# A CIN kernel on one core: joint squares for the first four chunks, second factors by shift matmuls for two chunks, another order of loads and of M

## The chip, the core and the metric

The kernel runs on one core of a Trainium2 chip. The metric is device time in microseconds (us), smaller is better. A time is one execution of the whole program; the profile is of one such execution.

## The reference

The input x has 1024 samples of 64 fields with 16 values each. Three layers of a compressed interaction network follow, all in float32. Without the dead branches the reference is:

```python
x0 = x; h = x; xs = []
for i in range(3):
    z = jnp.einsum('bfe,bge->bfge', x0, h)           # all products of fields
    z = z.reshape(Bn, f0 * fh, e)
    y = jnp.einsum('oc,bce->boe', Ws[i], z) + bs[i][None, :, None]
    if i != 2:
        x_i, h = y[:, :64, :], y[:, 64:, :]          # half is output, half goes on
    else:
        x_i, h = y, y
    xs.append(x_i)
pooled = jnp.sum(jnp.concatenate(xs, axis=1), axis=2)   # sum over the 16 values
out = pooled @ fc_w.T + fc_b                            # 256 -> 1
```

W0 is 128 x 4096, W1 and W2 are 128 x 4096 too. The output has 1024 numbers.

## The kernel before

**Tiling.** The 1024 samples are cut into 32 chunks of 32 samples; a chunk has 512 columns (32 samples by 16 values). The products of two fields are formed with the pair of fields on 128 partitions. Since a product of fields is symmetric, 16 tiles of 128 pairs and one tile of squares are enough. Tile t = 4j + i multiplies `xa` (the fields shifted by i, 128 partitions x 4 x 512) with `xb[j]` (the fields shifted by 4(j+1) and, in the lower half, by 16 more). `product(c, j)` forms four tiles `z` at once in one VectorE (DVE) instruction of 128 x 2048; in the last j, ScalarE (ACT) then overwrites a part of one tile with squares (line 220). A few products go to GpSimd (POOL).

**Weights.** Only half of W0 (64 output rows) is needed for h1; the output of the last layers is linear, so the kernel multiplies fc_w into W2 first (v2, lines 378 to 398), then v2 into W1 (the matrix M, `pm`, lines 404 to 414), writes M to HBM (`md`) and reads it back in skewed forms (`ms`), so that DVE can add the two halves of each symmetric pair into `w_all` (line 499). `w_all` holds for each tile 64 columns for h1 (W0) and 64 for M. For a chunk after the first four, TensorE (PE) contracts both at once (128 columns, 512 wide, `contract`, line 256). The first four chunks come before M is there: PE contracts them with the h1 columns first (`half_contract(c, 0, j)`, line 291: 64 columns, the chunk's two halves of 256 columns in two column tiles) and with the M columns later (`half_contract(c, 1, j)`).

**The head.** `HEAD = [2, 3, 0, 1]`, and c0, c1, c2, c3 stand for these four chunks in this order. The last two of them, `KEPT = [0, 1]`, keep their products in SBUF and get their second contraction right after the head; the first two are loaded and multiplied again later. Nothing is scheduled by a planner: `manual_schedule` keeps the order of the program text on each engine, and each engine runs its instructions in order. Loads are issued in the text's order on one queue, SyncE's (SP); DMAs issued on ACT are named in the text.

In the head before the change:

- For c0, the second factors `xp` come from eight small matmuls with a shift matrix (line 189), 64x64 tiles of 512 columns, into PSUM. For c1 they are loaded from HBM as `xb` (1 MB), and ACT copies three of the four to PSUM (line 178).
- c0's first product is one instruction for tile 0 and one for tiles 1 to 3; POOL forms the product j = 1 of c0 and j = 3 of c1.
- W0's two halves are added by DVE (`h1_weights`, line 339). For j = 0 and 1, ACT first copies one half to PSUM (line 355).
- Each chunk has a fifth step `half_contract(c, 0, NJ)` of the remaining squares: ACT squares 64 partitions (`squares`, line 224), and two matmuls with 64 rows add them to h1. Then ACT copies h1 with its bias to `hb` (`keep_h1`, line 297). For the kept chunks ACT also prepares the last tile and xx (`last_tile`, lines 224, 230 and 239) between c1 and c2.
- The order of PE's work is: c0; first quarter of c1; v2's first step (`pv`); fourth quarter of c1; v2's second step (`pt`); second and third quarters of c1; `pm`; squares of c1; c2; c3; then the kept chunks with M.

SP's loads are issued as: xa of c0 (in two parts), W0 (in two parts), xb and xa of c1, W2, xa and xb of c2, W1, and, once c0's buffer is free, xa and xb of c3.

The PSUM tags are `acc` (four banks), `y` and `set` (two each). `zp` has 12 buffers of `z`; `xp` has three of `xa` and of `xb`.

Of the kernel before, what the change touches and what calls it, by code (L numbers as in the profile page):

```python
# [36 lines left out]
F32 = mybir.dt.float32  # L37
AF = mybir.ActivationFunctionType
# [3 lines left out]
F = 64  # L42
# [15 lines left out]
FIRST = 4  # L58
SQ = slice(96, 128)
# [3 lines left out]
def cin_kernel(ctx, tc, xra, xrb, wh, w0r, w1h, w2t, wx1, wx0, vec, out):  # L63
    nc = tc.nc
# [26 lines left out]
    fc2, bh1, bh2 = vs[:, 0:1], vs[:, 1:2], vs[0:64, 2:3]  # L91
    bcol, fcol, fcb = vs[:, 3:5], vs[:, 5:7], vs[0:2, 7:8]
    w0ds, fcr = vs[:, 8:72], vs[:, 72:200]
# [4 lines left out]
    bd = const_tile("bd", [128, 128])  # L98
    nc.gpsimd.memset(bd, 0.0)  # L99

    def keep_clock(n):
        pw = ps.tile([128, 128], F32, tag="acc", name=f"pw_{n}", bufs=4)
        for _ in range(n):
            nc.tensor.matmul(pw, bd, bd, start=True, stop=True)  # L104

    keep_clock(6)

    shift = const_tile("shift", [128, 96])
    nc.gpsimd.memset(shift, 0.0)
    for base in (0, 64, -64):  # L110
        nc.gpsimd.affine_select(
            out=shift, in_=shift, compare_op=ALU.not_equal, fill=1.0, base=base,
# [15 lines left out]
    w_all = const_tile("w_all", [128, NT + 1, 192])  # L128
# [7 lines left out]
    def load_xa(c, at=slice(0, NI)):  # L136
        if c not in xas or at.start == 0:
            xas[c] = xp.tile([128, NI, N], F32, tag="xa", name=f"xa_{c}")
        nc.sync.dma_start(
            out=xas[c][:, at, :],  # L140
            in_=bass.AP(
                tensor=xra.tensor, offset=c * XR * N + at.start * N,
                ap=[[N, 128], [1, (at.stop - at.start) * N]],
            ),
        )

    def load_xb(c):
# [14 lines left out]
    nc.sync.dma_start(out=w0t[:, 0, :], in_=wh)  # L162
    nc.sync.dma_start(out=w0t[:, 1:NJ, :], in_=w0r)
    w0s = [w0t[:, j, :].rearrange("p (i v g) -> p i v g", v=2, g=F) for j in range(NJ)]
    xb0 = xp.tile([128, NJ, N], F32, tag="xb", name=f"xb_{c0}")[:, 0, :]
    load_xb(c1)
    load_xa(c1)
    for k in range(2):
        nc.sync.dma_start(out=w2s[k], in_=w2t[k])
    load_chunk(c2)  # L170
    nc.sync.dma_start(out=w1s, in_=w1h)

    def to_psum(src, tag, name):
        t = ps.tile(list(src.shape), F32, tag=tag, name=name, bufs=4 if tag == "acc" else 2)
        nc.scalar.copy(t, src)
        return t

    xbs[c0] = [
        ps.tile([128, N], F32, tag=tag, name=f"xp_{c0}_{j}", bufs=4 if tag == "acc" else 2)
        for j, tag in enumerate(("y", "y", "set", "acc"))
    ]
    for j in (0, 2):
        for r in range(2):
            for h in range(2):
                at = 4 * (j + r + 1) + 16 * h
                nc.tensor.matmul(  # L189
                    xbs[c0][j + r][halves[h]], shift[halves[r], at : at + F],  # L190
                    xas[c0][halves[r], 0, :], start=True, stop=True,
                )
    keep_clock(8)


# [1 line left out]
    hb = const_tile("hb", [128, NF, N // 2])  # L197
    accs, uus, zs, ys, parts = {}, {}, {}, {}, {}

    def new_acc(c, n=N):  # L200
        if c == NCH - 1:
            parts[c] = [
                (ps.tile([128, H2], F32, tag=tag, name=f"acc_{c}_{n}", bufs=bufs), cols)
                for n, (tag, bufs, cols) in enumerate(
                    (("acc", 4, slice(0, H2)), ("set", 2, slice(H2, N)))
                )
            ]
            return
        accs[c] = ps.tile([128, n], F32, tag="acc", name=f"acc_{c}", bufs=4)

    def product(c, j, first=0, last=NI, engine=nc.vector):
        if first == 0:
            zs[c, j] = z_tile(f"z_{c}_{j}")
        at = slice(first, last)
        engine.tensor_tensor(  # L215
            zs[c, j][:, at, :], xas[c][:, at, :],
            xbs[c][j].unsqueeze(1).to_broadcast([128, last - first, N]), ALU.mult,
        )
        if j == NJ - 1:
            nc.scalar.activation(zs[c, j][SQ, 0, :], xas[c][SQ, 0, :], AF.Square)  # L220

    def squares(c):
        zls[c] = xp.tile([128, N], F32, tag="zl", name=f"zl_{c}", bufs=4)
        nc.scalar.activation(zls[c][0:64], xas[c][0:64, 0, :], AF.Square)  # L224

    def last_tile(c):

        if c < FIRST:
            squares(c)
            nc.scalar.copy(zls[c][64:128], xas[c][64:128, 0, :])  # L230
        else:
            if c % 4 == 0:
# [51 lines left out]
    def half_contract(c, part, j):  # L284

        cols = slice(part * F, (part + 1) * F)
        rows = slice(0, F) if part == 0 and j == NJ else slice(0, 128)
        for t in (NT,) if j == NJ else [j * NI + i for i in tiles(j)]:
            z = zls[c] if t == NT else zs[c, j][:, t % NI, :]
            for n in range(2):  # L290
                nc.tensor.matmul(  # L291
                    accs[c][halves[n]], w_all[rows, t, cols], z[rows, n * H2 : (n + 1) * H2],
                    start=(t == 0), stop=(t == NT),
                )

    def keep_h1(c):
        nc.scalar.activation(hb[:, HEAD.index(c), :], accs[c], AF.Identity, bias=bh1)

    def uu_tile(k):
        if k not in uus:  # L300
# [37 lines left out]
    def h1_weights(j, other=None):  # L338
        nc.vector.tensor_tensor(  # L339
            w_all[:, j * NI : (j + 1) * NI, 0:64], w0s[j][:, :, 0, :],  # L340
            w0s[j][:, :, 1, :] if other is None else other, ALU.add,
        )


    new_acc(c0, H2)
    squares(c0)
    nc.vector.tensor_copy(w_all[0:32, NT, 0:64], w0ds[0:32])
    product(c0, 0, 0, 1)
    product(c0, 0, 1, NI)
    nc.scalar.copy(xb0, xbs[c0][1])  # L350
    xbs[c0][1] = xb0
    product(c0, 1, engine=nc.gpsimd)
    w0p = ps.tile([128, 2, NI, F], F32, tag="set", name="w0p")
    for j in range(2):
        nc.scalar.copy(w0p[:, j], w0s[j][:, :, 1, :])
        h1_weights(j, w0p[:, j])
    product(c0, 2)
    h1_weights(2)
    nc.vector.memset(w0s[3][SQ, 0, 1, :], 0.0)
    h1_weights(3)  # L360
    for j, tag in enumerate(("y", "y", "acc")):
        xbs[c1][j] = to_psum(xbs[c1][j], tag, f"xp_{c1}_{j}")
    product(c0, 3)
    for j in range(NJ + 1):
        half_contract(c0, 0, j)


    for j in range(NJ - 1):
        product(c1, j)
    product(c1, NJ - 1, engine=nc.gpsimd)  # L370
    keep_h1(c0)
    squares(c1)
    load_chunk(c3)
    new_acc(c1, H2)
    half_contract(c1, 0, 0)


    v2r = flat_tile("v2r")[:, 0:1024].rearrange("p (n c) -> p n c", n=2)
    v2t = const_tile("v2t", [128, F])
    for n in range(2):  # L380
        pv = ps.tile([128, 512], F32, tag="set", name=f"pv2_{n}")
        for k in range(4):
            nc.tensor.matmul(  # L383
                pv[32 * k : 32 * k + 32], fv2, w2s[n][:, k * 512 : (k + 1) * 512],
                start=True, stop=True,
                tile_position=(0, 32 * k),
            )
        nc.scalar.copy(v2r[:, n, :], pv)

    half_contract(c1, 0, 3)  # L390


    pt = ps.tile([128, F // 4, 4], F32, tag="acc", name="pt", bufs=4)
    v2q = v2r.rearrange("p n (s o) -> p (n s) o", o=F)
    for q in range(F // 4):
        for to in halves:
            nc.tensor.matmul(pt[to, q, :], v2q[:, q, :], pick, start=True, stop=True)  # L397
    nc.scalar.copy(v2t, pt.rearrange("p q k -> p (q k)"))
    half_contract(c1, 0, 1)

    half_contract(c1, 0, 2)


    m_sb = z_tile("m_sb")
# [8 lines left out]
    for m in (0, 2, 1, 3):  # L413
        nc.scalar.copy(m_sb[:, m, :], pms[m])  # L414

    half_contract(c1, 0, NJ)

# [20 lines left out]
    )  # L438


    keep_h1(c1)
    squares(c2)
    for c in KEPT:
        last_tile(c)

    new_acc(c2, H2)
    for j in range(NJ):
        product(c2, j)
    for j in range(NJ + 1):
        half_contract(c2, 0, j)  # L450


# [27 lines left out]
        read_rows(slice(1, NJ), queue, half)  # L480


    keep_h1(c2)
    new_acc(c3, H2)
    for j in range(NJ):
        product(c3, j)
    for j in range(NJ + 1):
        half_contract(c3, 0, j)

    for j in range(1, NJ):  # L490
# [7 lines left out]
        at = slice(j * NI, (j + 1) * NI)  # L498
        nc.vector.tensor_tensor(w_all[:, at, 64:128], ms[:, 0, at], ms[:, 1, at], ALU.add)  # L499

    keep_h1(c3)


    for j in range(NJ):
# [7 lines left out]


    for c in KEPT:
        new_acc(c, H2)
        for j in range(NJ):
            half_contract(c, 1, j)

# [214 lines left out]
```

## Time and profile before

| what | us |
|---|---|
| median of three runs | 494.91 |
| lowest, highest | 494.75, 495.42 |
| run with the profile | 494.79 |
| span in that profile | 493.0 |
| first product of c2 starts on DVE | 24.63 |
| second contraction of the kept chunks starts on PE | 47.34 |
| chunk 4 starts on PE | 61.31 |

The span goes from the first to the last instruction. The page gives each engine's busy time; the timeline lists instructions in order of time, those alike that follow each other as one row, with the start, the length, and in brackets how long the engine had been idle and what ended that. PE shows two records for each of these float32 matmuls. The end of a matmul in a record is modelled and overlaps the next start, so starts are what is compared. The DMA engines moved 401 to 423 GB/s between 8.45 and 30.58 us. The granted TensorE clock is 1.0 throughout.

### The profile page before, as it was taken

Reading aid. Unit: us, or ns where it says so; the run is one execution under the profiler, and the core shown is the slowest. Engines: PE = TensorE matmul, PEld = TensorE weight load, DVE = VectorE, ACT = ScalarE, POOL = GpSimd, SP = SyncE. Lnnn points to the kernel's source line nnn. Section 1 sums busy time; section 2 is a strip of 40 time slices with the busy share of each in tenths; the row PEclk is TensorE's granted clock in tenths of the full one; section 3 lists DMA queues with packets and bytes.
Section 4 is the critical chain, followed back from the end, with each engine's and each line's share of the span. In section 5 each row is a group of like instructions: output and inputs, shape, how many; then the busy total and the mean of one; then the engine's idle time right before and its main releaser. Section 6 shows DMA issues by size and latency. Waiting matters only on the chain.

```text
span 493.0 us, 4322 instructions
## 1 busy us (share of the span) xinstructions
PE 485.9 (99%) x1804; PEld 229.5 (47%) x1804; DVE 369.1 (75%) x232; ACT 93.0 (19%) x161; POOL 11.4 (2%) x20
## 2 busy tenths in 40 slices
PE   8998999999999999999999999999999999999996
PEld 5555644344644344443444444443444434444474
DVE  4795599998889988898768677776877676780311
ACT  3343012022111131212110021112011121010001
POOL 5300000000000000000000000000000000000000
PEclk9999999999999999999999999999999999999999
DMA  8986994174444453547133444333344430000000
GB/s 341 418 268 150 414 419 183 55 283 175 170 171 170 170 215 127 191 191 281 72 126 163 171 170 169 112 143 109 150 170 171 170 149 21 1 0 0 0 1 1
DMA packets 14243, 79.65 MB, mean 162 GB/s; under 512 B 3756, under 2 KB 4428, under 8 KB 4944
## 3 DMA queue, kind: packets, MB, share of 16 engines
q1 hardware_dynamic: 13084, 78.10, 40.9%
q10 hardware_dynamic: 1140, 1.29, 1.0%
q8 instruction: 14, 0.23, 0.2%
q14 instruction: 5, 0.04, 0.0%
HBM read 77.74 MB, written 1.64 MB: 161 GB/s over the span
## 4 chain that ended last, share of the span: by engine, by line
PE 94%; ACT 2%; DVE 1%; DMA 1%; ACTq 0%; SPq 0%; issue 0%
PE acc L256 78%; PE acc L291 10%; PE acc L275 3%; PE acc L266 2%; DMA w0t<-in_w0r 1%; DVE z L215 1%; ACT m_sb L414 0%; PE po L586 0%; PE y L324 0%; PE pv L383 0%; PE pt L397 0%; ACT zl L224 0%; ACT zl L230 0%; ACTq L432 0%; DVE w_all L339 0%; ACT xx L239 0%
## 5 line engine op out<-in xcount | busy, mean ns | idle before, releaser
L256 PE MATMUL acc<-z,w_all 128*128 128x512 f32 (+1 forms) x928 | 387.6, 579 | 0.0
L215 DVE TENSOR_TENSOR z<-xa,xb 128x2048 f32<-128x2048 f32 x128 | 287.6, 2285 | 46.7 <-PE acc L256 37.9
L256 PEld LDWEIGHTS acc<-z,w_all 128*128 128x128 f32 x928 | 175.6, 190 | 209.9 <-issue 206.3
L220 ACT ACTIVATE z<-xa 32x512 f32<-32x512 f32 x34 | 21.3, 626 | 320.1 <-DVE z L215 317.3
L318 DVE SCALAR_TENSOR_TENSOR uu<-acc,vs,q 64x512 f32<-64x512 f32 (+1 forms) x29 | 21.2, 732 | 61.3 <-ACT q L317 61.0
L291 PE MATMUL acc<-z,w_all 128*64 128x256 f32 x512 | 58.1, 381 | 2.1 <-ACT z L220 1.3
L291 PEld LDWEIGHTS acc<-z,w_all 128*64 128x64 f32 x512 | 35.9, 137 | 24.1 <-issue 4.1
L317 ACT COPY q<-acc 64x512 f32<-64x512 f32 (+1 forms) x29 | 16.4, 565 | 36.5 <-PE acc L256 22.9
L331 DVE TENSOR_REDUCE acc<-uu 128x64 f32<-128x1024 f32 (+3 forms) x20 | 20.5, 1026 | 0.4
L239 ACT COPY xx<-xa 64x512 f32<-64x512 f32 x32 | 19.6, 613 | 0.4
L235 ACT ACTIVATE sq<-xa 32x512 f32<-32x512 f32 x28 | 17.6, 628 | 4.3 <-DMA xa<-in_xra 3.6
L215 DVE TENSOR_TENSOR z<-xa,xp 128x2048 f32<-128x2048 f32 (+2 forms) x7 | 13.5, 1976 | 1.3 <-PE xp L189 1.3
L280 PE MATMUL y<-xx,bd 64*64 64x512 f32 x56 | 13.6, 604 | 0.0
L275 PE MATMUL acc<-xx,v1w 64*64 64x512 f32 (+1 forms) x58 | 13.5, 587 | 0.0
L327 DVE SCALAR_TENSOR_TENSOR uu<-y,cx,xx 128x512 f32<-128x512 f32 x16 | 11.3, 745 | 0.3
L215 POOL TENSOR_TENSOR z<-xa,xb 128x2048 f32<-128x2048 f32 x2 | 9.1, 4558 | 5.7 <-ACT xb L350 3.0
L266 PE MATMUL acc<-sq,w_sq 32*128 32x512 f32 (+1 forms) x58 | 8.0, 623 | 0.0
L275 PEld LDWEIGHTS acc<-xx,v1w 64*64 64x64 f32 x58 | 3.6, 132 | 8.9 <-issue 8.8
L104 PE MATMUL pw<-bd 128*128 128x128 f32 x28 | 5.0, 347 | 1.0 <-POOL bd L99 1.0
L104 PEld LDWEIGHTS pw<-bd 128*128 128x128 f32 x28 | 4.5, 251 | 1.8 <-POOL bd L99 1.0
L499 DVE TENSOR_TENSOR w_all<-ms 128x256 f32<-128x256 f32 x4 | 1.6, 424 | 4.8 <-DMA ms<-md 4.8
L266 PEld LDWEIGHTS acc<-sq,w_sq 32*128 32x128 f32 x58 | 2.6, 183 | 5.4 <-issue 5.3
(62 smaller groups left out, 66.6 us busy)
## 6 DMA issues: line engine op xcount, KB each, us to landing
xb<-in_xrb SPq DMA_DIRECT2D x33, 1024.0 KB, 6.9
xa<-in_xra SPq DMA_DIRECT2D x33, 1024.0 KB, 4.8
w<-in_w2t SPq DMA_DIRECT2D x2, 1024.0 KB, 12.4
w1s<-in_w1h SPq DMA_DIRECT2D x1, 1024.0 KB
w1x<-in_wx SPq DMA_DIRECT2D x1, 1024.0 KB, 9.6
w0x<-in_wx SPq DMA_DIRECT2D x1, 1024.0 KB, 10.1
xa<-in_xra SPq DMA_DIRECT2D x1, 768.0 KB, 4.7
w0t<-in_w0r SPq DMA_DIRECT2D x1, 768.0 KB, 6.4
```

Of the source, the lines that this page charges most:

```text
L215: engine.tensor_tensor(zs[c, j][:, at, :], xas[c][:, at, :], xbs[c][j].unsqueeze(1).to_broadcast([128, last - first, N]), ALU.mult,)
L220: nc.scalar.activation(zs[c, j][SQ, 0, :], xas[c][SQ, 0, :], AF.Square)
L235: nc.scalar.activation(sqs[c // 4][at : at + 32], xas[c][0:32, 0, :], AF.Square)
L239: nc.scalar.copy(xxs[c // 2][to], xas[c][to, 0, :])
L256: nc.tensor.matmul(acc_c, w_all[:, t, w_cols(c)], zs[c, j][:, i, cols], start=(t == 0 and c % 4 < 2), stop=(t == NT - NI and c % 4 >= 2),)
L266: nc.tensor.matmul(acc_c, w_sq[at, w_cols(c)], sqs[first // 4][at, cols], start=(r >= 2), stop=(r < 2), tile_position=(32 * r, 0),)
L275: nc.tensor.matmul(acc_c[q], v1w[rows], xxs[k][rows, cols], start=False, stop=(c % 4 < 2), skip_group_check=True,)
L280: nc.tensor.matmul(ys[k][rows], bd[rows, rows], xxs[k][rows], start=True, stop=True)
L291: nc.tensor.matmul(accs[c][halves[n]], w_all[rows, t, cols], z[rows, n * H2 : (n + 1) * H2], start=(t == 0), stop=(t == NT),)
L317: nc.scalar.copy(q[h, cols], acc_c[64 - h.start : 128 - h.start])
L318: nc.vector.scalar_tensor_tensor(uu[:, cols], acc_c[h], bh1[h], q[h, cols], ALU.add, ALU.mult)
L331: nc.vector.tensor_reduce(acc[rows, of, k, half], uus[k][rows, of, E * half.start : E * half.stop].rearrange("p k (b e) -> p k b e", e=E), ...
```

## The change

- The squares of the four head chunks are no longer a fifth step of each. ACT squares 32 partitions of each chunk into one quarter of a shared tile, `sq_head` (`head_square`), and after c3's first contraction eight matmuls with 32 rows and 64 columns each (`keep_h1`), at row tile 32r and column tile 64n, add them to all four h1 sums. The four copies to `hb` follow there, and then the kept chunks' `last_tile`. The h1 sums stay in the four `acc` banks until then; the kept chunks' second sums use tag `y`.
- c1's second factors come from shift matmuls too, placed after c0's first quarter, in PSUM tiles of tags `y` and `set`. The load of c1's xb is gone; ACT copies one factor to SBUF for POOL. c1's xa is loaded in two parts.
- W1 is loaded before c2's xa and xb.
- v2's first step stands ahead of c1's first quarter, and `pm` after c1's first and fourth quarters, ahead of the second and third.
- c0's product j = 0 is cut into tiles 0, 1 and 2 to 3, with `h1_weights(0)` in between. ACT copies a half of W0 to PSUM for all four j, the last two into `misc`, the bank in which `keep_clock` runs.
- Without use, and removed: the copy of `w0ds` into `w_all`, and the case of 64 rows in `half_contract`.

```diff
-    xb0 = xp.tile([128, NJ, N], F32, tag="xb", name=f"xb_{c0}")[:, 0, :]
-    load_xb(c1)
-    load_xa(c1)
+    xb_gps = xp.tile([128, NJ, N], F32, tag="xb", name="xb_gps")
+    load_xa(c1, slice(0, 1))
+    load_xa(c1, slice(1, 4))
     for k in range(2):
         nc.sync.dma_start(out=w2s[k], in_=w2t[k])
+    nc.sync.dma_start(out=w1s, in_=w1h)
     load_chunk(c2)
-    nc.sync.dma_start(out=w1s, in_=w1h)
...
+    sq_head = xp.tile([128, N], F32, tag="zl", name="sq_head", bufs=4)
+    h1_accs = {}
+
+    def head_square(c):
+        at = 32 * HEAD.index(c)
+        nc.scalar.activation(sq_head[at : at + 32], xas[c][0:32, 0, :], AF.Square)
...
+    def keep_h1():
+        for r, c in enumerate(HEAD):
+            at = slice(32 * r, 32 * r + 32)
+            for n in range(2):
+                nc.tensor.matmul(
+                    h1_accs[c][halves[n]], w0ds[at], sq_head[at, n * H2 : (n + 1) * H2],
+                    start=False, stop=True, tile_position=(32 * r, 64 * n),
+                )
+        for c in HEAD:
+            nc.scalar.activation(
+                hb[:, HEAD.index(c), :], h1_accs[c], AF.Identity, bias=bh1
+            )
...
-    product(c0, 0, 0, 1)
-    product(c0, 0, 1, NI)
...
+    product(c0, 0, 0, 1)
+    product(c0, 0, 1, 2)
+    nc.scalar.copy(w0o[0], w0s[0][:, :, 1, :])
+    h1_weights(0, w0o[0])
+    product(c0, 0, 2, NI)
+    nc.scalar.copy(w0o[1], w0s[1][:, :, 1, :])
+    h1_weights(1, w0o[1])
     product(c0, 2)
-    h1_weights(2)
-    nc.vector.memset(w0s[3][SQ, 0, 1, :], 0.0)
-    h1_weights(3)
-    for j, tag in enumerate(("y", "y", "acc")):
-        xbs[c1][j] = to_psum(xbs[c1][j], tag, f"xp_{c1}_{j}")
+    for j in (2, 3):
+        nc.scalar.copy(w0o[j], w0s[j][:, :, 1, :])
+    nc.vector.memset(w0o[3][SQ, 0, :], 0.0)
+    for j in (2, 3):
+        h1_weights(j, w0o[j])
+    half_contract(c0, 0, 0)
+
+    head_acc(c1)
+    for j, tag in ((0, "y"), (1, "y"), (3, "set"), (2, "set")):
+        shifted(c1, j, tag)
+    shift_pair(c1, (0, 1))
+    shift_pair(c1, (3, 2))
+    nc.scalar.copy(xb_gps[:, 1, :], xbs[c1][3])
+    xbs[c1][3] = xb_gps[:, 1, :]
+    head_square(c1)
+
     product(c0, 3)
-    for j in range(NJ + 1):
+    load_chunk(c3)
+    for j in range(1, NJ):
         half_contract(c0, 0, j)
...
-    keep_h1(c0)
-    squares(c1)
-    load_chunk(c3)
-    new_acc(c1, H2)
-    half_contract(c1, 0, 0)
...
-    half_contract(c1, 0, 3)
+    half_contract(c1, 0, 0)
...
-    half_contract(c1, 0, 1)
-
-    half_contract(c1, 0, 2)
+    half_contract(c1, 0, 3)
...
-    half_contract(c1, 0, NJ)
+    for j in (1, 2):
+        half_contract(c1, 0, j)
...
-    keep_h1(c1)
-    squares(c2)
-    for c in KEPT:
-        last_tile(c)
-
-    new_acc(c2, H2)
+    head_square(c2)
+    head_acc(c2)
     for j in range(NJ):
         product(c2, j)
-    for j in range(NJ + 1):
+    for j in range(NJ):
         half_contract(c2, 0, j)
...
-    keep_h1(c3)
+    keep_h1()
+    for c in KEPT:
+        last_tile(c)
...
     for c in KEPT:
-        new_acc(c, H2)
+        new_acc(c, H2, "y")
```

More of the change, by code (lines that the diff above doesn't have):

```diff
@@ L99, in cin_kernel @@
     nc.gpsimd.memset(bd, 0.0)
+    misc = ps.tile([128, N], F32, tag="acc", name="misc", bufs=4)
     def keep_clock(n):
-        pw = ps.tile([128, 128], F32, tag="acc", name=f"pw_{n}", bufs=4)
         for _ in range(n):
-            nc.tensor.matmul(pw, bd, bd, start=True, stop=True)
+            nc.tensor.matmul(misc[:, 0:128], bd, bd, start=True, stop=True)
     keep_clock(6)
@@ L164, in cin_kernel, with shifted, shift_pair @@
     w0s = [w0t[:, j, :].rearrange("p (i v g) -> p i v g", v=2, g=F) for j in range(NJ)]
-    xb0 = xp.tile([128, NJ, N], F32, tag="xb", name=f"xb_{c0}")[:, 0, :]
-    load_xb(c1)
-    load_xa(c1)
+    xb_gps = xp.tile([128, NJ, N], F32, tag="xb", name="xb_gps")
+    load_xa(c1, slice(0, 1))
+    load_xa(c1, slice(1, 4))
     for k in range(2):
         nc.sync.dma_start(out=w2s[k], in_=w2t[k])
+    nc.sync.dma_start(out=w1s, in_=w1h)
     load_chunk(c2)
-    nc.sync.dma_start(out=w1s, in_=w1h)
[L176 to L186, printed above, removed]
+    def shifted(c, j, tag):
+        xbs.setdefault(c, {})[j] = ps.tile(
+            [128, N], F32, tag=tag, name=f"xp_{c}_{j}", bufs=4 if tag == "acc" else 2
+        )
+    def shift_pair(c, js):
+        for r, j in enumerate(js):
             for h in range(2):
-                at = 4 * (j + r + 1) + 16 * h
+                at = 4 * (j + 1) + 16 * h
                 nc.tensor.matmul(
-                    xbs[c0][j + r][halves[h]], shift[halves[r], at : at + F],
-                    xas[c0][halves[r], 0, :], start=True, stop=True,
-                )
+                    xbs[c][j][halves[h]], shift[halves[r], at : at + F],
+                    xas[c][halves[r], 0, :], start=True, stop=True,
+                )
+    for j, tag in enumerate(("y", "y", "set", "acc")):
+        shifted(c0, j, tag)
+    shift_pair(c0, (0, 1))
+    shift_pair(c0, (2, 3))
     keep_clock(8)
@@ L198, in cin_kernel, with new_acc @@
     accs, uus, zs, ys, parts = {}, {}, {}, {}, {}
-    def new_acc(c, n=N):
+    def new_acc(c, n=N, tag="acc"):
         if c == NCH - 1:
@@ L208, in new_acc @@
             return
-        accs[c] = ps.tile([128, n], F32, tag="acc", name=f"acc_{c}", bufs=4)
+        accs[c] = ps.tile([128, n], F32, tag=tag, name=f"acc_{c}", bufs=4 if tag == "acc" else 2)
     def product(c, j, first=0, last=NI, engine=nc.vector):
@@ L286, in half_contract @@
         cols = slice(part * F, (part + 1) * F)
-        rows = slice(0, F) if part == 0 and j == NJ else slice(0, 128)
         for t in (NT,) if j == NJ else [j * NI + i for i in tiles(j)]:
@@ L291, in half_contract, with head_acc @@
                 nc.tensor.matmul(
-                    accs[c][halves[n]], w_all[rows, t, cols], z[rows, n * H2 : (n + 1) * H2],
+                    accs[c][halves[n]], w_all[:, t, cols], z[:, n * H2 : (n + 1) * H2],
                     start=(t == 0), stop=(t == NT),
                 )
-    def keep_h1(c):
-        nc.scalar.activation(hb[:, HEAD.index(c), :], accs[c], AF.Identity, bias=bh1)
+    sq_head = xp.tile([128, N], F32, tag="zl", name="sq_head", bufs=4)
[3 more added lines that the diff above has]
+        nc.scalar.activation(sq_head[at : at + 32], xas[c][0:32, 0, :], AF.Square)
+    def head_acc(c):
+        new_acc(c, H2)
+        h1_accs[c] = accs[c]
+    def keep_h1():
[9 more added lines that the diff above has]
+                hb[:, HEAD.index(c), :], h1_accs[c], AF.Identity, bias=bh1
+            )
     def uu_tile(k):
@@ L342, in h1_weights @@
         )
-    new_acc(c0, H2)
-    squares(c0)
-    nc.vector.tensor_copy(w_all[0:32, NT, 0:64], w0ds[0:32])
-    product(c0, 0, 0, 1)
-    product(c0, 0, 1, NI)
-    nc.scalar.copy(xb0, xbs[c0][1])
-    xbs[c0][1] = xb0
+    head_acc(c0)
+    head_square(c0)
+    nc.scalar.copy(xb_gps[:, 0, :], xbs[c0][1])
+    xbs[c0][1] = xb_gps[:, 0, :]
     product(c0, 1, engine=nc.gpsimd)
     w0p = ps.tile([128, 2, NI, F], F32, tag="set", name="w0p")
-    for j in range(2):
-        nc.scalar.copy(w0p[:, j], w0s[j][:, :, 1, :])
-        h1_weights(j, w0p[:, j])
-    product(c0, 2)
-    h1_weights(2)
-    nc.vector.memset(w0s[3][SQ, 0, 1, :], 0.0)
-    h1_weights(3)
-    for j, tag in enumerate(("y", "y", "acc")):
-        xbs[c1][j] = to_psum(xbs[c1][j], tag, f"xp_{c1}_{j}")
+    w0q = misc.rearrange("p (j i g) -> p j i g", i=NI, g=F)
+    w0o = [w0p[:, 0], w0p[:, 1], w0q[:, 0], w0q[:, 1]]
+    product(c0, 0, 0, 1)
[5 more added lines that the diff above has]
+    h1_weights(1, w0o[1])
+    product(c0, 2)
+    for j in (2, 3):
[12 more added lines that the diff above has]
+    head_square(c1)
     product(c0, 3)
-    for j in range(NJ + 1):
+    load_chunk(c3)
+    for j in range(1, NJ):
         half_contract(c0, 0, j)
@@ L380, in cin_kernel @@
     for n in range(2):
-        pv = ps.tile([128, 512], F32, tag="set", name=f"pv2_{n}")
+        pv = ps.tile([128, 512], F32, tag=("y", "set")[n], name=f"pv2_{n}")
         for k in range(4):
@@ L388, in cin_kernel @@
         nc.scalar.copy(v2r[:, n, :], pv)
-    half_contract(c1, 0, 3)
-    pt = ps.tile([128, F // 4, 4], F32, tag="acc", name="pt", bufs=4)
+    half_contract(c1, 0, 0)
+    pt = ps.tile([128, F // 4, 4], F32, tag="y", name="pt")
     v2q = v2r.rearrange("p n (s o) -> p (n s) o", o=F)
@@ L480, in cin_kernel @@
         read_rows(slice(1, NJ), queue, half)
-    keep_h1(c2)
-    new_acc(c3, H2)
+    head_square(c3)
+    head_acc(c3)
     for j in range(NJ):
         product(c3, j)
-    for j in range(NJ + 1):
+    for j in range(NJ):
         half_contract(c3, 0, j)
```

## The prediction

> **What bounds the kernel now.** I read the busy line of the page first, then the list of waits of PE, then the timeline of PE over the head of the kernel.
>
> ```profile
> PE 485.9 (99%) x1804; PEld 229.5 (47%) x1804; DVE 369.1 (75%) x232; ACT 93.0 (19%) x161; POOL 11.4 (2%) x20
> ```
>
> PE is busy for 485.9 of 493.0 us. The waits of PE (total, times, longest) say where the rest is:
>
> ```profile
> PE acc L291 <- ACT z L220: 1.3, 1, 1.3
> ...
> PE acc L291 <- POOL z L215: 0.6, 1, 0.6
> PE acc L291 <- DVE z L215: 0.2, 1, 0.2
> ```
>
> The two lines left out are the first microsecond and 1.5 us of the tail (line 586), which the change does not touch. All three waits shown lie in the head. PE timeline (start, length, line, records; PE stands at two records per matmul):
>
> ```profile
> 8.47 1.95 PE L291 MATMUL acc<-z,w_all 128*64 128x256 f32 x16
> 10.97 3.67 PE L291 MATMUL acc<-z,w_all 128*64 128x256 f32 x32 [0.56 <-POOL z L215]
> 14.89 1.95 PE L291 MATMUL acc<-z,w_all 128*64 128x256 f32 x16 [0.24 <-DVE z L215]
> 16.77 0.65 PE L291 MATMUL acc<-zl,w_all 64*64 64x256 f32 x4
> 17.35 1.95 PE L291 MATMUL acc<-z,w_all 128*64 128x256 f32 x16
> 19.22 1.93 PE L383 MATMUL pv<-w,fv 128*32 128x512 f32 x16
> 21.08 1.95 PE L291 MATMUL acc<-z,w_all 128*64 128x256 f32 x16
> 22.86 1.98 PE L397 MATMUL pt<-pick,v2r 128*64 128x4 f32 x64
> 24.69 3.65 PE L291 MATMUL acc<-z,w_all 128*64 128x256 f32 x32
> 28.27 1.95 PE L409 MATMUL pm<-w1s,v2t 64*64 64x512 f32 x16
> 30.04 0.61 PE L291 MATMUL acc<-zl,w_all 64*64 64x256 f32 x4
> 30.58 6.70 PE L291 MATMUL acc<-z,w_all 128*64 128x256 f32 x60
> 38.55 0.65 PE L291 MATMUL acc<-z,w_all 128*64 128x256 f32 x4 [1.27 <-ACT z L220]
> 39.13 0.65 PE L291 MATMUL acc<-zl,w_all 64*64 64x256 f32 x4
> 39.71 7.13 PE L291 MATMUL acc<-z,w_all 128*64 128x256 f32 x64
> 46.77 0.65 PE L291 MATMUL acc<-zl,w_all 64*64 64x256 f32 x4
> 47.34 14.03 PE L291 MATMUL acc<-z,w_all 128*64 128x256 f32 x128
> ```
>
> A quarter of a contraction (16 records) is 1.78 us from start to start (21.08 to 22.86); the last matmul's end is drawn later, so I count starts. From 47.34 to the tail PE never waits. So the head decides: whatever moves the start at 47.34 moves the end, as long as the others keep ahead. Those others, DVE in the head, and the row tiles of line 266 in the chain of waits:
>
> ```profile
> 24.63 17.70 DVE L215 TENSOR_TENSOR z<-xa,xb 128x2048 f32<-128x2048 f32 x8 [3.20 <-DMA xb<-in_xrb]
> 43.61 0.43 DVE L499 TENSOR_TENSOR w_all<-ms 128x256 f32<-128x256 f32 x1 [1.28 <-DMA ms<-md]
> ...
> 47.17 0.76 DVE L499 TENSOR_TENSOR w_all<-ms 128x256 f32<-128x256 f32 x2 [3.14 <-DMA ms<-md]
> ```
>
> ```profile
> 90.64 1.07 PE acc L266 x8
> ```
>
> The products of c2 and c3 start when c2's second factor lands at 24.63 and run without a gap to 42.33. The weights made from M (line 499) are done at 44.0 for the first quarter, 47.6, 47.9 and 48.8 for the others.
>
> **What the Trainium skill says.** "TensorEngine Tiling (Array Packing)", Available Configurations, lists a mode of 32x64 with eight independent tiles, which is the shape of the new squares; its Key Properties say that a change of tiling mode drains TensorE. The trace agrees with both as far as it goes: four 32x128 tiles of 512 columns take 1.07 us, where one full 128x512 matmul takes 0.86 (27.66 us for 64 records from 93.58), and a square step is 0.57 where two column tiles of 256 columns stream in 0.44. Its Gotcha 1 asks that row tiles write different PSUM banks; the four h1 sums are four tiles of a bank each. "DMA: Bandwidth & Descriptors", Queues, rings and completion order, says each DMA engine takes descriptors in ring order. The trace agrees: successive 1 MB loads on SP's queue end 2.5 us apart (11.04 and 13.64), so a landing is set by the bytes ahead of it.
>
> **The change, part by part, on PE's line from 8.47 to 47.34 (38.87 us).**
>
> Removed, squares: four steps of 0.58, 0.54, 0.58 and 0.57 us, 2.27.
>
> Removed, waits, as start to start minus the quarters inside: 10.97-8.47-1.78 = 0.72; 14.89-10.97-3.56 = 0.36; for c2 39.13-30.58-7.06 = 1.49 (7.06 is c3's, 39.71 to 46.77). Together 2.57. The first two were the wait for POOL's product and for c0's last product on DVE; now eight shift matmuls stand ahead of those quarters, so both operands (POOL 10.92, DVE 14.85) are there in time. The third was ACT: at 33.4 it ran one h1 copy (0.47), two squares, and the two kept chunks' six further instructions of 0.6 before the square in c2's last product, 37.87. Now ACT has only one 0.63 square there and the last product's own square runs at 33.5, when DVE ends, long before PE asks (about 36).
>
> Added, eight shift matmuls for c1, after c0's first quarter, 10.25. Nearest row: line 409, the same 64x64 tiles of 512 columns, 1.77 us (28.27 to 30.04); the first use at line 189 took 2.33 (4.07 to 6.40). Their xa piece is 256 KB behind the 2 MB that land at 8.55, so about 9.2: in time. The pair for j = 2 takes the PSUM tile that c0's product 2 reads until 11.66 (it starts at 9.38 as before, behind the same weights). Pairs (0,1) run 10.25 to 11.13, j = 3 from 11.13, j = 2 from 11.7 to 12.6. I take 2.35 us; bounds 1.8 and 2.9. Queued behind that wait are c0's quarters 1 to 3; their readers come later.
>
> Added, the joint squares: eight 32x64 tiles of 256 columns. Line 266 is 0.21 us above one matmul; with 0.43 for one and some 0.3 for issue and drain, 0.75. Bounds: 0.5 and 1.07.
>
> Added, changes of tiling mode at new places, 0.1; bounds 0 and 0.4.
>
> Sum: -2.27-2.57+2.35+0.75+0.10 = -1.64 us. The bounds of the costs give -2.5 to -0.5.
>
> Moved at no cost, with what hides it. M: v2's matmuls now stand ahead of c1's first quarter and pm ahead of two quarters more, so pm ends at about 27.0 instead of 30.0 and its copies, writes and reads move with it by nearly 3 us, SP's and ACT's issues of them too. The weights are needed at 45.7, 47.5, 49.3; even at the old times (44.0, 47.6, 47.9) only 0.1 would be lost. W1 goes ahead of c2's two loads on SP's queue, but c1's xb (1 MB) is gone and c1's xa is two issues for one: the bytes ahead of c2's xb are 8 MB before and after, so it should still land near 24.6, and W1 near 19, wanted at 25. c3's loads wait for the same release (15.57). Two extra copies of W0 on ACT (0.38 each) lie in its gap at 9.0 to 11.0, the split of c0's first product costs DVE 0.1 in its gap before 9.05. POOL's second product waits for ACT's copy at 12.7 instead of the DMA at 13.64 and ends by 17.5, wanted at 23.4. The four h1 copies (1.9), the six copies and squares of the kept chunks (3.7) and the weight copies (1.4) now follow 45.7 on ACT and end near 52.7, when ACT had waited for xa until 52.80 anyhow; SP's load of the sixth chunk, behind the first kept chunk's copies, goes at 49.4, against 49.58. DVE loses one 0.18 copy. Later margins at a PE 1.64 us sooner: first z of chunk 4 is ready at 57.6, wanted at 59.7; V1's weights 69.8 against 73.6; V0's 86.2 against 90.0.
>
> The floor: c3's last product ends at 42.33, then one quarter (1.78) and the squares (0.75) must follow, so the second parts cannot start before 44.9. That caps the gain at 2.4; the path above gives 45.7.
>
> The profiled run was 494.79 us with a span of 493.0; the others 494.75 to 495.42, median 494.91. The span would be 491.4, the time 494.91-1.64 = 493.3 us. About 0.2%, 0.99 us, is what a measurement of this kernel can tell from no change.
>
> **Rivals.** (1) The gain is larger: no wait at the j = 2 shift and cheap mode changes, up to the floor, 492.5. For it: the pairs may overlap the wait; against: the PSUM tile is busy until 11.66. It is a tail of the forecast.
>
> (2) A landing takes the place of the waits. c2's xb or M's reads come 1 to 2 us later than I count, since DMA runs at 401 to 423 GB/s in this stretch and W1 now stands in front. The floor is then the bound: every microsecond of landing after 25.4 costs one, and at 27.0 nothing is left. At 26.4 the gain is 0.6: 494.3. Against: the bytes ahead are equal.
>
> (3) Slower: the eight squares run one after another. Place: the end of c3's first part. Price: 8 x 0.43 = 3.4 us instead of 0.75, so -1.64+2.7 = +1.05: 496.0. It decides against the change from 2.4 us on for this step. For it: no row shows 32x64 tiles; against: row tiles overlap at line 266 and column tiles in every quarter.
>
> **How the numbers follow.** The forecast with rival 1, its upper tail, has 0.80, rival 2 has 0.12, rival 3 or another loss 0.08. The weakest part of the forecast (a gain of 0.5 to 0.99 us) would count as no change, and about as much of rival 2 would still be over the mark. So faster 0.80, same 0.12, slower 0.08. The range runs from the floor, 492.5, to 494.6, which takes in the weak bound of the costs and rival 2 at 0.6, and leaves out rival 3 and a landing later than 26.7.
>
> **What would show it.** In the profile after: no wait of PE on ACT near 37; a shift step of about 2.3 us at 10.3 with a wait of some 0.5 on DVE; pm ending near 27.0 and the first kept quarter starting near 45.7; the joint squares under 1.1 us; c2's first product still at 24.6. The prediction is wrong if that product starts after 25.4, if PE waits for line 528 or for chunk 4's products, or if the squares take over 2 us.

## The result, and the profile after

The changed kernel takes 492.77 us (median of six runs, 492.56 to 493.09), the kernel before 494.88 beside it: 2.11 us less, a ratio of 0.9957 with a 95% interval of 0.9944 to 0.9969. The forecast was 493.3. The span of the profiled run fell from 493.0 to 491.0.

The busy line of the page after shows that PE's busy time is 0.2 us more than before: shifts have come in for the squares. The 2 us came out of its idle time, 7.1 us of the span before and 4.9 after.

```profile
PE 486.1 (99%) x1820; PEld 229.6 (47%) x1820; DVE 369.1 (75%) x232; ACT 93.2 (19%) x162; POOL 11.4 (2%) x20
```

The whole list of PE's waits after (total, times, longest). The three of line 291 are gone, and none took their place:

```profile
PE po L617 <- DVE acc L354: 1.5, 1, 1.5
PE misc L105 <- POOL bd L99: 1.0, 1, 1.0
```

The timeline of PE after, from the first quarter on:

```profile
9.03 1.95 PE L292 MATMUL acc<-z,w_all 128*64 128x256 f32 x16
10.91 1.95 PE L186 MATMUL xp<-xa,shift 64*64 64x512 f32 x16
12.79 5.40 PE L292 MATMUL acc<-z,w_all 128*64 128x256 f32 x48
18.12 1.92 PE L417 MATMUL pv<-w,fv 128*32 128x512 f32 x16
19.97 1.95 PE L292 MATMUL acc<-z,w_all 128*64 128x256 f32 x16
21.75 1.98 PE L431 MATMUL pt<-pick,v2r 128*64 128x4 f32 x64
23.59 1.93 PE L292 MATMUL acc<-z,w_all 128*64 128x256 f32 x16
25.44 1.95 PE L441 MATMUL pm<-w1s,v2t 64*64 64x512 f32 x16
27.32 17.49 PE L292 MATMUL acc<-z,w_all 128*64 128x256 f32 x160
44.74 0.69 PE L313 MATMUL acc<-sq_head,vs 32*64 32x256 f32 x16
45.35 14.03 PE L292 MATMUL acc<-z,w_all 128*64 128x256 f32 x128
```

The second contraction starts at 45.35 instead of 47.34, 1.99 us sooner, and the end follows by the same amount. Ten quarters run without a break from 27.32 to 44.74; the joint squares take 0.61 us (44.74 to 45.35). The timeline of DVE after:

```profile
24.70 17.71 DVE L217 TENSOR_TENSOR z<-xa,xb 128x2048 f32<-128x2048 f32 x8 [3.50 <-DMA xb<-in_xrb]
42.32 0.42 DVE L528 TENSOR_TENSOR w_all<-ms 128x256 f32<-128x256 f32 x1
44.03 0.43 DVE L528 TENSOR_TENSOR w_all<-ms 128x256 f32<-128x256 f32 x1 [1.28 <-DMA ms<-md]
45.13 0.76 DVE L528 TENSOR_TENSOR w_all<-ms 128x256 f32<-128x256 f32 x2 [0.67 <-DMA ms<-md]
```

c2's second factor lands when it did (24.63 before), and the four additions that make M's weights (line 499 before, 528 here) start 1.3 to 3.1 us sooner.

### The profile page after: what moved, and what is told of

It is laid out like the page before. It is cut to its first block, busy times and chain, and to the rows that moved or that the text cites. A ratio compares the mean times of both kernels' runs of the same rounds, so it can differ in the third digit from the quotient of the medians.

```text
span 491.0 us, 4356 instructions
## 1 busy us (share of the span) xinstructions
PE 486.1 (99%) x1820; PEld 229.6 (47%) x1820; DVE 369.1 (75%) x232; ACT 93.2 (19%) x162; POOL 11.4 (2%) x20
## 3 DMA queue, kind: packets, MB, share of 16 engines
HBM read 76.69 MB, written 1.64 MB: 160 GB/s over the span
## 4 chain that ended last, share of the span: by engine, by line
PE 99%; DVE 0%; ACT 0%; issue 0%; POOL 0%; POOLq 0%
PE acc L258 79%; PE acc L292 12%; PE acc L277 3%; PE acc L268 2%; PE xp L186 1%; PE misc L105 1%; PE po L617 0%; PE y L347 0%; PE pm L441 0%; PE pv L417 0%; PE pt L431 0%; PE y L282 0%; PE acc L313 0%; DVE uu L341 0%; DVE acc L354 0%
## 5 line engine op out<-in xcount | busy, mean ns | idle before, releaser
L217 POOL TENSOR_TENSOR z<-xa,xb_gps 128x2048 f32<-128x2048 f32 x2 | 9.1, 4565 | 5.6 <-ACT xb_gps L370 3.2
L105 PE MATMUL misc<-bd 128*128 128x128 f32 x28 | 5.0, 347 | 1.0 <-POOL bd L99 1.0
L105 PEld LDWEIGHTS misc<-bd 128*128 128x128 f32 x28 | 4.5, 250 | 2.2 <-issue 1.2
L186 PE MATMUL xp<-xa,shift 64*64 64x512 f32 x32 | 5.2, 784 | 0.0
```

Of the source, the lines that this page charges most:

```text
L105: nc.tensor.matmul(misc[:, 0:128], bd, bd, start=True, stop=True)
L217: engine.tensor_tensor(zs[c, j][:, at, :], xas[c][:, at, :], xbs[c][j].unsqueeze(1).to_broadcast([128, last - first, N]), ALU.mult,)
```

## Experiments

All ratios are to the kernel before, measured beside it. Each time is the median of 5 to 21 executions, and each kernel has one profile. Three dots stand for lines that are not shown; a diff shows the lines that matter, not every one.

**The changed kernel again.** No edit.

> The changed kernel once more, beside the other: 492.8 within 0.3. TensorE's first shifts run partly at half speed; where the speed-up falls may differ from run to run, so the first quarter may start between 8.4 and 9.4 instead of at 9.03, and the whole moves with it.

492.78 us, 0.9959 (0.9945 to 0.9972). Its PE timeline:

```profile
8.55 1.95 PE L292 MATMUL acc<-z,w_all 128*64 128x256 f32 x16
10.43 2.35 PE L186 MATMUL xp<-xa,shift 64*64 64x512 f32 x16
12.71 5.40 PE L292 MATMUL acc<-z,w_all 128*64 128x256 f32 x48
...
45.28 14.03 PE L292 MATMUL acc<-z,w_all 128*64 128x256 f32 x128
```

The first quarter starts 0.48 us sooner than in the other profile, but the shifts now take 2.28 us from start to start (10.43 to 12.71) instead of 1.88, and the next quarter starts within 0.08 us of the other. I had expected the whole to move with the first quarter, and here it does not: the wait of the pair j = 2 for its PSUM tile takes up the difference.

**The joint squares alone.** The kernel before with `head_square`, `head_acc` and the joint `keep_h1`, and the PSUM tags these need.

```diff
-    for j in range(NJ + 1):
+    for j in range(NJ):
         half_contract(c0, 0, j)
...
-    keep_h1(c3)
+    keep_h1()
+    for c in KEPT:
+        last_tile(c)
```

> The kernel before with the joint squares alone: no squares step per chunk, one step of eight small tiles after c3, the h1 copies and the kept chunks' last tiles after it; the shifts for c1, W1's place and M's order stay as before. Theory (the head's line on PE, part by part): 2.27 of squares and the 1.49 wait on ACT go, 0.61 comes, the two waits of 0.72 and 0.36 stay. PE's path would reach the second contraction at about 44.2, the floor of DVE (24.65 + 17.7 + 1.75 + 0.61) allows 44.7, and the second quarter then waits for M's weights until about 47.0, so the effect is that of a start near 45.2: 492.8 us, as much as the whole change. Rival (each part of the change brings its share, the shifts and the earlier M among them): 493.3 to 493.7.

493.48 us, 0.9972 (0.9961 to 0.9983): 1.41 us less than before. Its PE timeline around the second contraction:

```profile
42.74 1.95 PE L292 MATMUL acc<-z,w_all 128*64 128x256 f32 x16 [0.25 <-DVE z L216]
44.62 0.69 PE L312 MATMUL acc<-sq_head,vs 32*64 32x256 f32 x16
45.23 1.95 PE L292 MATMUL acc<-z,w_all 128*64 128x256 f32 x16
47.92 12.31 PE L292 MATMUL acc<-z,w_all 128*64 128x256 f32 x112 [0.74 <-DVE w_all L513]
```

It reaches the second contraction at 45.23, as soon as the whole change does, and then waits for M's weights: 47.92 - 45.23 - 1.75 = 0.94 us (1.75 is a quarter of this stretch, 13.97 us for eight before), since M was no sooner than before. The theory's numbers give 47.0 - 44.71 - 1.75 = 0.54. Its direction holds (DVE's products and M's weights become the bound), its size does not: the squares bring two thirds of the gain, and the time lies in the middle of what the rival gave.

**Everything but the joint squares.** The changed kernel with the squares step, h1 copy and last tile of each chunk where they were.

```diff
-    head_square(c2)
-    head_acc(c2)
+    keep_h1(c1)
+    squares(c2)
+    for c in KEPT:
+        last_tile(c)
+    new_acc(c2, H2)
...
-    for j in range(NJ):
+    for j in range(NJ + 1):
         half_contract(c2, 0, j)
```

> The changed kernel without the joint squares: each head chunk has its own squares step, h1 copy and (the kept chunks) last tile where the kernel before had them; the shifts for c1, W1's place, M's order and the split of W0's halves stay as changed. Theory (by the line on PE): 2.27 of squares come back for 0.61, the second contraction starts at 47.0 instead of 45.35, with no wait on ACT near c2 since pm and ACT's work are 3 us sooner than before: 494.4. So the rest of the change alone is worth 0.3 to 0.5, the squares alone 1.4 and both 2.1. Rival (ACT's long run between c1 and c2 makes PE wait as before): 495.0 to 496.0.

494.75 us, 0.9997 (0.9989 to 1.0005): no change from before can be told. Its PE timeline:

```profile
12.59 5.40 PE L293 MATMUL acc<-z,w_all 128*64 128x256 f32 x48
...
31.88 7.13 PE L293 MATMUL acc<-z,w_all 128*64 128x256 f32 x64
38.94 0.65 PE L293 MATMUL acc<-zl,w_all 64*64 64x256 f32 x4
...
47.16 14.03 PE L293 MATMUL acc<-z,w_all 128*64 128x256 f32 x128
```

There is no wait on ACT in c2, from 31.88 to 38.94. ACT's long run comes sooner with M (the square in c2's last product runs at 36.47 instead of 37.87), and PE comes to c2 1.3 us later than before (31.88 against 30.58):

```profile
36.47 0.63 ACT L222 ACTIVATE z<-xa 32x512 f32<-32x512 f32 x1
```

But the shifts cost what the waits had. The difference of 0.13 from before cannot be told from none; the squares alone bring 1.41, both parts 2.10: some 0.56 us exist only together. The likely reason is that the squares need the earlier M, for which they waited 0.94 us above; no run gives them the earlier M without the shifts.

The changed kernel, measured beside this one, is 1.97 us faster, where the prediction's own terms (2.27 less 0.61 measured) give 1.66. A removed step thus cost (1.97 + 0.61)/4 = 0.645 us on average, not the 0.57 from its start to the next. The starts agree: from quarter 1 to the second contraction PE takes 34.57 us here (12.59 to 47.16) and 32.56 in the changed kernel (12.79 to 45.35), 2.01 less, so 0.655 a step.

**M's order undone.** The changed kernel with v2's steps and `pm` in the order of before.

```diff
+    half_contract(c1, 0, 0)
...
     for n in range(2):
...
-    half_contract(c1, 0, 0)
...
+    half_contract(c1, 0, 3)
...
-    half_contract(c1, 0, 3)
...
+    for j in (1, 2):
+        half_contract(c1, 0, j)
     m_sb = z_tile("m_sb")
...
-    for j in (1, 2):
-        half_contract(c1, 0, j)
```

> The changed kernel with M's steps in the order of before (v2's first step after c1's first quarter, its second after the fourth, pm after all four quarters). PE has the same work. Theory (M's order matters because the second contraction now starts at 45.35): pm ends near 30.9 instead of 27.3, M's weights for quarters 1 to 3 come 3.6 us later, at 48.1 to 49.4 where PE asks for the first of them at 47.1: a wait of 1.0 to 1.5 us, 494.0. Rival (what the prediction said of the old times, that M's order is worth 0.1): 492.9.

495.18 us, 1.0006 (0.9998 to 1.0014): 2.4 us more than the changed kernel. Neither number was right. PE:

```profile
46.05 0.65 PE L292 MATMUL acc<-z,w_all 128*64 128x256 f32 x4 [1.38 <-ACT z L222]
...
49.79 12.31 PE L292 MATMUL acc<-z,w_all 128*64 128x256 f32 x112 [0.59 <-DVE w_all L531]
```

The wait for the weights is there (0.59), but a larger one ahead of it, 1.38 us, comes from ACT. ACT's timeline in the same kernel:

```profile
34.91 0.63 ACT L222 ACTIVATE z<-xa 32x512 f32<-32x512 f32 x1
42.59 0.50 ACTq L502 DMA_DIRECT2D ms<-md  x1
43.18 0.78 ACTq L496 DMA_DIRECT2D ms<-md  x1
43.99 0.69 ACTq L502 DMA_DIRECT2D ms<-md  x1
44.72 0.63 ACT L303 ACTIVATE sq_head<-xa 32x512 f32<-32x512 f32 x1 [9.19 <-issue]
45.38 0.62 ACT L222 ACTIVATE z<-xa 32x512 f32<-32x512 f32 x1
```

ACT issues part of M's reads, and each waits in ACT's queue until M is written, here to 42.59. In the changed kernel the first of these reads goes out at 37.49. Behind them stand the square of c3 and the square in c3's last product, which DVE had finished at 42.5. DVE's line for the weights of quarters 1 and 2 tells which of the two waits sets the end:

```profile
49.31 0.91 DVE L531 TENSOR_TENSOR w_all<-ms 128x256 f32<-128x256 f32 x2 [2.23 <-DMA ms<-md]
```

The weights of quarter 1 wait for their reads until 49.31, and PE goes on at 49.79, when they are made. The reads that they need stand ahead of the two squares in ACT's queue, or on SP's. So without the wait on ACT, PE would only have waited longer for the weights: the late M alone accounts for the 2.4 us, as the theory said, with the weights 1.6 us later than it had put them (49.7 against 48.1). The 1.38 us lie inside that.

**No shifts.** The changed kernel with c1's factors loaded, three of them copied to PSUM by ACT as before; W1 stays ahead of c2.

```diff
+    load_xb(c1)
     load_xa(c1, slice(0, 1))
     load_xa(c1, slice(1, 4))
...
-    shift_pair(c1, (0, 1))
-    shift_pair(c1, (3, 2))
...
+        nc.scalar.copy(t, xbs[c1][j])
...
```

> The changed kernel without the shift matmuls for c1: its second factors are loaded (1 MB, ahead of c1's xa) and copied to PSUM by ACT as before; W1 still goes ahead of c2's loads. Theory (a landing is set by the bytes ahead of it, and DVE's eight products after it are a floor): c2's second factor lands at 27.2 instead of 24.7, c3's last product ends at 44.9, the second contraction starts at about 47.3, time 494.8, though PE has 1.88 us less work. Rival (the PE work counts, the landing does not): second contraction at 44 to 45, 491.5 to 492.5.

495.34 us, 1.0010 (1.0001 to 1.0018). First its DVE timeline, then its PE timeline:

```profile
27.39 17.71 DVE L218 TENSOR_TENSOR z<-xa,xb 128x2048 f32<-128x2048 f32 x8 [6.24 <-DMA xb<-in_xrb]
```

```profile
19.92 1.06 PE L416 MATMUL pv<-w,fv 128*32 128x512 f32 x8 [2.00 <-DMA w<-in_w2t]
...
45.16 1.95 PE L293 MATMUL acc<-z,w_all 128*64 128x256 f32 x16 [0.26 <-DVE z L218]
47.03 0.69 PE L314 MATMUL acc<-sq_head,vs 32*64 32x256 f32 x16
47.65 14.03 PE L293 MATMUL acc<-z,w_all 128*64 128x256 f32 x128
```

One megabyte more ahead of c2's factor makes it land 2.7 us later, and a kernel with 1.88 us less PE work is 2.6 us slower than the changed one. PE also waits 2.00 us for W2, which the same megabyte delays, but this does not set the end: the last quarters of the first contraction wait for DVE, so DVE's products after the late landing do. The theory holds; its time was 0.5 us too low. This is the second rival of the prediction, brought about: the shifts pay by the bytes that they save. That these bytes make room for the early W1 is argued; no run loads c1's factors with W1 behind c2.

**W1 late.** The changed kernel with W1 loaded after c2.

```diff
-    nc.sync.dma_start(out=w1s, in_=w1h)
     load_chunk(c2)
+    nc.sync.dma_start(out=w1s, in_=w1h)
```

> The changed kernel with W1 loaded after c2's xa and xb, as before. Theory: c2's products start near 22.2 instead of 24.7, but PE's own line sets the second contraction (45.35), and W1 lands about 24.8, before its use at 25.4: no change, 492.8 within 0.2. Rival (DVE's floor after the landing is what binds in the changed kernel): start 0.5 sooner, 492.3. Second rival (W1 late delays M and PE): 493.2 or more.

493.01 us, 0.9960 (0.9947 to 0.9973). First DVE, then PE:

```profile
22.59 17.70 DVE L217 TENSOR_TENSOR z<-xa,xb 128x2048 f32<-128x2048 f32 x8 [1.15 <-DMA xb<-in_xrb]
```

```profile
9.22 1.95 PE L292 MATMUL acc<-z,w_all 128*64 128x256 f32 x16
...
45.54 14.03 PE L292 MATMUL acc<-z,w_all 128*64 128x256 f32 x128
```

DVE is 2.1 us ahead and PE gains nothing; the second contraction starts 0.19 later only because the first quarter does (9.22 against 9.03). In the changed kernel PE's own line is the bound, and W1's place is worth nothing by itself.

**One filler.**

```diff
-    keep_clock(8)
+    keep_clock(1)
```

> The changed kernel with one filler matmul instead of eight after the first shifts. In the profile after, the weights of the first quarter are ready at 7.48 and its first product at 7.2, but the fillers hold PE until 9.03. Theory: the first quarter starts at 7.6, waits for its third and fourth tile until 8.6, ends near 9.5, the shifts follow and the pair j = 2 waits for PSUM until 11.5; quarter 1 starts at 12.4 instead of 12.79, the second contraction at 44.95, 492.4 us. Rival (the fillers hold TensorE's fast clock): PE falls back or warms later, the first quarter runs at half speed, 492.8 to 494.

492.70 us, 0.9957 (0.9943 to 0.9971), no change. PE:

```profile
7.51 2.22 PE L292 MATMUL acc<-z,w_all 128*64 128x256 f32 x16 [0.42 <-DVE w_all L362]
9.66 3.13 PE L186 MATMUL xp<-xa,shift 64*64 64x512 f32 x16
12.72 5.40 PE L292 MATMUL acc<-z,w_all 128*64 128x256 f32 x48
```

The weight loads of the last pair of shifts (PEld, TensorE's weight loads) name the wait:

```profile
11.71 0.20 PEld L186 LDWEIGHTS xp<-xa,shift 64*64 64x64 f32 x4 [1.00 <-DVE z L217]
```

The first quarter starts 1.5 us sooner, and the shifts then take 3.06 us: the pair j = 2 cannot start before DVE has read c0's factor from the same PSUM tile (product 2 runs from 9.38 to 11.66 here). Quarter 1 starts at 12.72, not at the 12.4 I expected. The matmuls of the first quarter, where none waits, start 0.21 us apart with one filler as with eight, so its pace does not need the fillers here.

**One row tile.** The four chunks' squares on the same 32 partitions, each in a tile of its own.

```diff
-                    h1_accs[c][halves[n]], w0ds[at], sq_head[at, n * H2 : (n + 1) * H2],
-                    start=False, stop=True, tile_position=(32 * r, 64 * n),
+                    h1_accs[c][halves[n]], w0ds[at], sq_heads[c][at, n * H2 : (n + 1) * H2],
+                    start=False, stop=True, tile_position=(0, 64 * n),
```

> The changed kernel with the four head squares each on partitions 0 to 31 of a tile of its own, so that all eight small matmuls use the same row tile and only the two column tiles can overlap. Theory (row tiles are what runs together): the step takes 4 x 0.43 + 0.15 = 1.9 us instead of 0.61, the kernel 1.3 us longer, 494.1. Rival (the eight would have run in about 0.6 us anyway, issue-bound): 492.8, no change. If they ran with no overlap at all: 3.4 us, 495.6.

494.19 us, 0.9986 (0.9980 to 0.9993). PE:

```profile
44.77 1.94 PE L313 MATMUL acc<-sq_head,vs 32*64 32x256 f32 x16
46.64 14.03 PE L292 MATMUL acc<-z,w_all 128*64 128x256 f32 x128
```

1.87 us for the same eight matmuls: four pairs one after another. With four row tiles it is 0.61, so the eight tiles do run together, which the third rival denied.

**A mix.** c1's factors 0 and 1 from shifts, 2 and 3 loaded; W1 after c2; `pm` one quarter later; one filler.

```diff
     load_xa(c1, slice(0, 1))
+    nc.sync.dma_start(out=xb_gps[:, 2:4, :], in_=xrb[c1][:, 2:4, :])
     load_xa(c1, slice(1, 4))
...
-    shift_pair(c1, (3, 2))
```

> The changed kernel with four other choices: c1's factors j = 0, 1 from shifts and j = 2, 3 loaded (512 KB), W1 loaded after c2, pm behind one more quarter, one filler instead of eight. Theory (the shifts' wait for the PSUM tile of c0's product 2 until 11.5 hides what fewer fillers free, and DVE's floor is the next bound): shifts take 0.95 and wait for nothing, quarter 1 starts at 11.2 on POOL's product instead of 12.8, c2's factor lands near 23.4, the second contraction starts at 44.1, 491.5. Rival (DVE's products or W2's landing take over in c1): 492.3 to 493.

492.12 us, 0.9945 (0.9932 to 0.9957): faster than the kernel before, and 0.65 us below the changed one. The executions of the two do not overlap (492.05 to 492.29 against 492.56 to 493.09), but they were not timed side by side. PE:

```profile
9.78 1.09 PE L187 MATMUL xp<-xa,shift 64*64 64x512 f32 x8
11.30 5.51 PE L293 MATMUL acc<-z,w_all 128*64 128x256 f32 x48 [0.43 <-POOL z L218]
17.05 1.92 PE L417 MATMUL pv<-w,fv 128*32 128x512 f32 x16 [0.25 <-DVE z L218]
...
44.51 14.03 PE L293 MATMUL acc<-z,w_all 128*64 128x256 f32 x128
```

Quarter 1 starts 1.5 us sooner, on POOL's product, as expected; the second contraction 0.84 sooner instead of 1.25. The rest went into two waits, from start to start: 0.42 us of v2's step for c1's first product, and some 0.2 ahead of `pm`, which stands behind the semaphore of W1's load.

**The mix with eight fillers.** The same with `keep_clock(8)`.

> The same with eight fillers as in the changed kernel. Theory: the first quarter starts at 8.5 to 9.2 when the fillers end, quarter 1 at 11.2 to 12.0, the second contraction 0 to 0.7 us later than with one filler: 491.5 to 492.2. Rival (fewer fillers cost more by a slower TensorE clock than they free): faster than with one filler.

492.76 us, 0.9957 (0.9944 to 0.9969): slower than expected. PE has a wait that the mix with one filler does not have:

```profile
18.92 1.07 PE L417 MATMUL pv<-w,fv 128*32 128x512 f32 x8 [0.82 <-DMA w<-in_w2t]
```

Quarter 1 starts at 11.43 against 11.30, so the fillers themselves cost 0.13; the rest is W2, whose second half is used here when it has only just landed. Why it landed later than in the other kernel, in which no load differs, stays open. So the mix is faster than the changed kernel (492.77) only where W2 lands in time, and the rival, that fewer fillers cost more by a slower clock, is not what the times show.

## Why the prediction was right

**The bound.** The head sets the end, and only where the second contraction starts counts: right. Start and span moved by 1.99 and 2.0 us, and nothing was lost between 45.35 and the tail.

**The removed waits, 2.57.** Right; none came back. The reason given for the third, less work on ACT, is one of two: the kernel with all but the squares has no such wait either, because ACT's run comes sooner with M and PE comes later.

**The removed squares, 2.27.** Too small by about 0.3. I counted from the start of a step to the next start. TensorE changes its tiling mode on the way in as well: before, the quarter ahead of a squares step took 1.88 us (14.89 to 16.77) against 1.78. The Trainium skill, "TensorEngine Tiling (Array Packing)", Key Properties, which I had cited for the drain, covers both changes; I priced one. The traces agree: one, two, three, four and ten quarters up to a start in another shape take 1.88, 3.60, 5.33, 7.06 and 17.42 us (the two in the kernel with the squares apart, the four before, the others after), which is 1.73 each and 0.15 once. The way in is thus an estimated 0.15 us, and a step shares it where its neighbour changes the shape anyway. The measured difference puts a step at 0.645 us on average.

**The shifts, 2.35.** Right where the first quarter starts early (2.28 in the repeat), and right there on what bounds them: quarter 1 was put at 12.6 and came at 12.71 and 12.72 with the first quarter at 8.55 and 7.51. In the first profile after, it was otherwise: the first quarter started at 9.03, not at the 8.47 I took over from before, the shifts took 1.88, and the wait of some 0.5 on DVE that I had named as a sign was not there. That quarter 1 still came at 12.79 is partly luck, since 0.56 too late and 0.47 too short nearly cancel; where the first quarter started at 9.33 (M's order undone), it came at 13.08. That the pair j = 2 waits for its PSUM tile when PE is early is shown; that a shorter product 2 on DVE would bring it forward is only argued, as the mix took the pair away instead.

**The joint squares, 0.75.** Measured 0.61. The eight tiles overlap.

**Sum.** -1.64 predicted; with 0.31 for the other mode changes and 0.14 for the joint squares -2.09, less the 0.1 to 0.2 by which quarter 1 came later. Measured 1.99 and 2.06 (45.28 in the repeat) in the start, 2.11 in time. What is left, about 0.1, the times do not resolve. The starts leave out the first quarter: from quarter 1 to the second contraction the prediction has 33.1 us (12.6 to 45.7), and the changed kernel takes 32.56 in both profiles within 0.01. Of the 0.54, the joint squares are 0.14 and the removed squares 0.31 to 0.35. So the start was forecast 0.35 too late (45.7 against 45.35): 0.54 too much was counted after quarter 1, and quarter 1 came 0.19 late.

**M at no cost.** The move was right (pm's next step starts at 27.32; I had 27.0), but the remark that the old times would cost 0.1 was wrong in substance. With the shifts in front the old order does not give the old times: quarter 1's weights are made at 49.7 instead of 47.6. `pm` starts 0.9 us later (29.19 against 28.27), and the first of ACT's reads of M goes out 2.5 us later (42.59 against 40.06); why writing M takes longer there stays open. I also overlooked the squares that stand behind M's reads on ACT. The order is worth 2.4 us.

**The rivals.** The floor is real, as the last quarter with the joint squares alone waits for DVE (0.25 us at 42.74), but the change does not touch it: with c2's factor 2.1 us sooner nothing changed. A late landing does what the second rival said, when a megabyte is put in front; in the change as it is, the bytes are equal and it did not occur. The third is refuted by the kernel with one row tile. One reading was loose: the 11.04 and 13.64 given for the ends of two loads are the starts of the instructions that waited for them, 2.60 us apart, not 2.5; nothing in the sum rests on it.

## What to carry to other kernels

Price a small step in another tiling mode with the changes on both sides of it, and gather such steps: four in one place, on four row tiles, cost 0.61 us where they had cost some 2.6. When a step that feeds DMA reads is moved, look at what stands behind those reads in the issuing engine's queue: here it held PE for 1.38 us. But ask which wait ends last: the data came later still, so only the data counted. And a part that is worth nothing alone can carry the others: shifts, loads and M's order brought nothing that could be told alone and some 0.7 us on top of the squares.

## What the runs showed of the hardware

TensorE's first matmuls run at about half the later pace, and the moment of the speed-up varies. The eight first shifts begin between 3.85 and 4.07 us in all kernels. Four of their records start some 0.85 us after the four before them at first (0.52 with the squares alone) and some 0.42 later. All eight last from 1.90 us (squares alone, 3.85 to 5.75) to 3.49 us (M's order undone, 3.85 to 7.34). The first quarter of the changed kernel started at 9.03 in one profile and at 8.55 in the other. The Trainium skill, "TensorE: Matmul & The Clock Gate", What's actually happening, says that the activity window behind the speed-up runs freely and does not start with the kernel. A moment that differs between two executions of one kernel fits this; the window itself shows in no trace here. The granted clock on the page read 1.00 in these stretches all the same, so the slow phase is seen only in the spacing and lengths of the records.
